# 32-column tiles for layer 0's projections, adapters of experts 0 to 3 in the score banks, and padded FFN weights

## The chip, the cores and the metric

The kernel runs on one core of a Trainium2 chip. The metric is the device time of one execution in microseconds (us), less is better. The time before is the median of three runs; the profile is of one execution.

## The reference

Two post-norm transformer layers on x of 8 batches x 512 tokens x 512 features, all in fp32. Layer 0 has causal attention with 16 heads of 32 and a mixture of 8 experts (top 2 by a router), each with low-rank adapters of rank 16. Layer 1 has an attention with 8 query heads of 64 on 2 key/value heads, and a gated FFN with integer weights, 1408 hidden units.

```python
def _L0_attn_ref(x, WQ_w, WQ_b, WK_w, WK_b, WV_w, WV_b, WO_w, WO_b):
    q = (x @ WQ_w.T + WQ_b).reshape(b, s, NH, HD).transpose(0, 2, 1, 3)    # k and v likewise
    scores = jnp.einsum('bhqd,bhkd->bhqk', q, k) * (1.0 / math.sqrt(HD))
    scores = jnp.where(causal, -jnp.inf, scores)
    out = jnp.einsum('bhqk,bhkd->bhqd', jax.nn.softmax(scores, axis=-1), v)
    return out.transpose(0, 2, 1, 3).reshape(b, s, h) @ WO_w.T + WO_b

def _L0_ffn_ref(x, ...):
    router_logits = xf @ gate_weight.T + xf @ gate_delta.T          # gate_delta = 2 * B @ A
    routing_weights, selected = jax.lax.top_k(softmax(router_logits), 2)    # then normalised to sum 1
    gup = einsum('th,eho->teo', xf, gate_up_proj) + SCALING * einsum('ter,eor->teo', einsum('th,erh->ter', xf, gup_lora_A), gup_lora_B)
    gates, h = jnp.split(gup, 2, axis=-1)
    h = silu(gates) * h
    out = einsum('tei,eih->teh', h, down_proj) + SCALING * (the same with down_lora_A, down_lora_B)
    # the two selected experts' rows of out, weighted and summed

def _L1_ffn_ref(x, wq_gate, s_gate, wq_up, s_up, wq_down, s_down):   # W = (wq - 128) * scale
    return _qlinear(silu(_qlinear(x, wq_gate, s_gate)) * _qlinear(x, wq_up, s_up), wq_down, s_down)

x = layernorm(x + _L0_attn_ref(x, ...))
x = layernorm(x + _L0_ffn_ref(x, ...))
x = layernorm(x + _L1_attn_ref(x, ...))
x = layernorm(x + _L1_ffn_ref(x, ...))
```

## The kernel before

The kernel runs in four stages one after the other: attention of layer 0 (from the start to about 710 us), expert tiles (to about 1200 us), attention of layer 1 (to about 1675 us) and the FFN of layer 1 (to the end). They overlap somewhat at their ends.

**Attention of layer 0** (`attention0`). For each batch b there are four groups g of four heads, and for each group three units u, which take the key tiles {0}, {1, 3} and {2} of 128 keys. We write a unit as (g, u). A unit computes its scores (`scores`, L1386): four matmuls per key tile, one for each head, with 32 rows of weights each, so that each head uses 32 rows of TensorE's array ("32*128" in the profile: rows*columns of the weights). The result `sc` has four PSUM banks, one for each head, and there is one such buffer (`p_sc`, bufs=1). Causality leaves 512 - 128 kt query columns for key tile kt; unit 2 therefore fills 256 of the 512 columns of each bank. ScalarE takes the exponential (L1390), POOL masks the diagonal block (L1395). Then come the unit's other tasks ("thunks", below). Last comes the product with the values of the unit before (`product`, L1410): four matmuls with 32 columns of weights ("128*32"), one for each head, each to its own 32 partitions of `av`. With unit 1 comes `normalise` of the group before: the sums of the exponentials by matmuls with ones (`rs`, L1425, also 128*32), a copy on ScalarE (L1004), reciprocal and product on VectorE (L1428, L1429), a guard's sum on POOL (L1007).

The tasks are set out by `plan(b)`. For a batch in the middle they are values (`value`, L1294) in group 0, query and key (`query` L1301, `key` L1313) of the next group, and the output projection of the batch before (`project`, L1321), each four matmuls that accumulate over 128-row chunks, with 128*128 weights and 512 moving columns. There are also the router's products: `score` (logits, L491), `choose` (L503), `dispatch` (L547, L548) and `enter` (a table of tokens, L588, in bf16). They use two PSUM banks in turn (tag "mm"). For batches 1 to 6 unit (3,2) has, ahead of `score`, one `merge`, and unit (2,2) another.

A `merge` adds the adapters to one 512-column chunk of two experts' weights: two matmuls with 16 rows (`delta`, L781) to two "mm" banks, for each a copy on ScalarE with the factor 2 (`scaled`, L792) and an add on POOL (L794). `scaled` tiles share two buffers with `r_inv` of `normalise`. Of the 24 merges, 12 (experts 0 to 3) lie in batches 1 to 6, and 12 (experts 4 to 7) among the first expert tiles.

The order on TensorE is that of the program only where `in_order` is open: in the first few instructions, and from group 2 of the last batch on. In between, the framework's planner picks for each engine the first instruction of the program that its own estimate of the times calls ready, and a buffer of a tag is chosen when its first writer is planned.

**Attention of layer 1** multiplies in tiles of 64 columns (`Attention1.multiply`, L1600).

**FFN of layer 1** (`IntegerFfn`). For each batch, 11 chunks c of 128 hidden units. Gate and up (`hidden`, L1152) are 16 matmuls with 128*128 weights on two halves of x (a high and a low part in float32r), and down (`out`, L1168) has the hidden halves as weights and the down weights as moving data. The weights, 33 units of 512 columns, lie in two tiles `ffn_w`: the first has 20 units (gate and up of chunks 0 to 9), the second the rest. `IntegerWeights.open` allocates them, the first in the pool `c_weights` on the right side of SBUF, below `x_2` to `x_7`.

In the profile one fp32 matmul of the program is two records; a float32r or bf16 matmul is one.

Of the kernel before, what the change touches and what calls it, by code (L numbers as in the profile page):

```python
# [9 lines left out]
F32 = mybir.dt.float32  # L10
# [8 lines left out]
P = 128  # L19
NB = 8  # L20
# [33 lines left out]
V_BQ, V_BK, V_NS, V_SS, V_SG, V_SU = 0, 4, 8, 12, 16, 16 + NHID  # L54
N_VEC = 16 + 2 * NHID


# [359 lines left out]
class Router:  # L417
# [75 lines left out]

    def choose(self, b, parts, ps):

# [6 lines left out]
        for t in range(NT):  # L502
            nc.tensor.matmul(ps[:, t, :], lhsT=parts[:, ts(t, P)], rhs=self.gather, start=True, stop=True)  # L503
        pr = small.tile([P, NT, E], F32, name="pr")
# [37 lines left out]

    def dispatch(self, b, ps):

        nc, small = self.nc, self.small
        flat = "p t e -> p (t e)"
        nc.tensor.matmul(ps.rearrange(flat), lhsT=self.before, rhs=self.both.rearrange(flat), start=True, stop=False)  # L547
        nc.tensor.matmul(ps.rearrange(flat), lhsT=self.ones, rhs=self.earlier.rearrange(flat), start=False, stop=True)  # L548
        here = slice(NT * b, NT * (b + 1))
        parts = small.tile([P, TOP_K, NT], F32, name="parts")  # L550
        for k in range(TOP_K):
            for of_expert, out in ((ps, self.ranks[:, k, here]), (self.part, parts[:, k, :])):
                mine = small.tile([P, NT, E], F32, name="mine")
                nc.vector.tensor_tensor(mine, of_expert, self.hots[:, k, here, :], ALU.mult)
                nc.vector.tensor_reduce(out, mine, AX.X, ALU.add)
# [26 lines left out]

    def enter(self, ps, low, high, column):

        nc, n = self.nc, TOP_K * NT
        for h, part in enumerate((low, high)):
            for i in range(n):
                nc.tensor.matmul(ps[:, h, :], lhsT=part[:, i, :], rhs=column[:, i, :], start=i == 0, stop=i == n - 1)  # L588
        nc.vector.tensor_tensor(self.table, ps[:, 0, :], self.table, ALU.add)
        nc.vector.scalar_tensor_tensor(self.table, ps[:, 1, :], float(P), self.table, ALU.mult, ALU.add)  # L590
# [160 lines left out]
class Experts:  # L751
# [31 lines left out]
    def chunk(self, e, c, n=1):  # L783
        return self.by_expert[:, e : e + n, 512 * c : 512 * (c + 1)]

    def merge(self, e, c, ps, scaled):
# [436 lines left out]
def attention0(env, guard, keep, routes, experts, dram, p_mm, tiles_ctx):  # L1223
# [8 lines left out]
    with ExitStack() as phase:  # L1232
# [55 lines left out]
        def mm(shape, name):  # L1288
            return p_mm.tile(shape, F32, tag="mm", name=name)

        def value(b, t):
            ps = mm([P, D], "ps_v")
            for c in range(ND):
                nc.tensor.matmul(ps, lhsT=xts[b][:, c, ts(t, P)], rhs=wv[:, c, :], start=c == 0, stop=c == ND - 1)  # L1294
            vs[t] = own.tile([P, D], F32, tag=f"v{t}", name=f"v{t}")
            nc.vector.tensor_tensor(vs[t], ps, row[:, 0, :], ALU.add)

        def query(b, g):
            ps = mm([P, S], "ps_q")
            for c in range(ND):  # L1300
                nc.tensor.matmul(ps, lhsT=wq[:, g, ts(c, P)], rhs=xts[b][:, c, :], start=c == 0, stop=c == ND - 1)  # L1301
            q = own.tile([P, S], F32, tag="q", name="q", bufs=2)
# [7 lines left out]
        def key(b, g):  # L1310
            ps = mm([P, S], "ps_k")
            for c in range(ND):
                nc.tensor.matmul(ps, lhsT=wk[:, g, ts(c, P)], rhs=xts[b][:, c, :], start=c == 0, stop=c == ND - 1)  # L1313
# [4 lines left out]
        def project(b, t):  # L1318
            ps = mm([P, D], "ps_o")
            for c in range(ND):  # L1320
                nc.tensor.matmul(ps, lhsT=aoTs[b][:, c, ts(t, P)], rhs=wo[:, c, :], start=c == 0, stop=c == ND - 1)  # L1321
            nc.vector.tensor_tensor(xs[b][:, t, :], ps, xs[b][:, t, :], ALU.add)
# [38 lines left out]

        def choose(b):
            router.choose(b, logits.pop(b), mm([P, NT, E], "ps_r"))

        def dispatch(b, mm=mm):
            router.dispatch(b, mm([P, NT, E], "ps_rank"))

# [6 lines left out]

        def enter(rows, mm=mm):
            router.enter(mm([P, 2, E * E_TILES], "ps_table"), *rows)

        def scores(b, g, u):
            q, k = heads[b, g]
            sc = p_sc.tile([P, 4, S], F32, tag="sc", name="sc")  # L1380
            width = 0
            for kt in UNITS[u]:
# [6 lines left out]
            p = own.tile([P, 4, width], F32, tag=f"p{u}", name="p", bufs=2 if u == 0 else 1)  # L1389
            nc.scalar.activation(p, sc[:, :, :width], AF.Exp, scale=scale)  # L1390

            at = 0
# [38 lines left out]

        merges = [(e, c) for e in range(0, E, 2) for c in range(UPS)]

# [6 lines left out]
        def plan(b):  # L1440
# [11 lines left out]
            if b:  # L1452
# [10 lines left out]
                if not by_dma:  # L1463
                    todo[2, 2].append(lambda: choose(pb))
                if not last:
                    todo[2, 2 if by_dma else 1].append(merge)
                    todo[3, 2 if by_dma else 1].insert(0, merge)
            if b == 0:
# [75 lines left out]
        one_hot(b - 1, (0, 1))  # L1544
        project(b, 0)
        project(b, 1)
        rows = one_hot(b - 1, (2, 3))
        project(b, 2)
        project(b, 3)
        experts.load(7)  # L1550
        enter(rows)
        for _ in range(2):
# [6 lines left out]
        merge()  # L1559
        choose(b)  # L1560
        tiles.step()
        merge()
        dispatch(b, tiles.aside)
# [4 lines left out]
        enter(rows, tiles.aside)  # L1568
        tiles.of_fixed = router.fixed(routes)
# [7 lines left out]
class Attention1:  # L1577
# [19 lines left out]
    def multiply(self, b, out, lhsT, rhs, c):  # L1597

        for m in (slice(0, self.HD), slice(self.HD, P)) if b else (slice(0, P),):
            self.nc.tensor.matmul(out[m], lhsT=lhsT[:, m], rhs=rhs, start=c == 0, stop=c == ND - 1)  # L1600

# [266 lines left out]
def usual_pass(tc, ins, held_out):  # L1868
    nc = tc.nc
    with ExitStack() as ctx:  # L1870
# [4 lines left out]
        with tc.tile_pool(name="a_mm", bufs=2, space=PSUM) as p_mm, ExitStack() as attn1_ctx:  # L1875
# [339 lines left out]
```

## Time and profile before

| | before |
|---|---|
| median of three runs | 2182.87 us (2181.64 to 2183.12) |
| the profiled execution | 2183.3 us |
| its span | 2181.6 us |
| granted TensorE clock, mean | 0.997 |
| instructions in the span | 25149 |
| busy: TensorE matmul, VectorE, ScalarE, POOL | 2151.6, 1273.8, 627.5, 497.8 us |
| DMA, mean over the span | 89 GB/s |

The span runs from the first to the last instruction of the program; what lies around it belongs to the execution's time. The matmuls of the profile are pipelined: a record lasts longer than it takes to start the next, so records are read by their starts, and the busy time of a group is no price of one. PE is the matmul, PEld its load of weights. A line of the timeline merges neighbours of one kind; its second number is the time from the first one's start to the last one's end. What stands in brackets behind a line is idle time of that engine just before it, and what ended it.

### The profile page before, as it was taken

What the parts mean: (1) busy time and instruction counts of PE and PEld (TensorE: products, weight loads), DVE (VectorE), ACT (ScalarE), POOL (GpSimd) and SP (SyncE); (2) the same over time, 40 slices, a digit from 0 to 9 for tenths busy, and PEclk for the clock granted to TensorE, in tenths of its full rate; (3) what the DMA queues carried; (4) which work ended last, traced back from release to release, by engine and by line L of the source; (5) the groups of instructions that cost most, each with busy time, mean ns of one, the idle gap of its engine ahead of it and who ended that gap; (6) DMA issues with size and microseconds to landing.
All of it is one profiled execution on the core that took longest, in us unless ns stands there. A gap on an engine that the chain in (4) does not pass through costs nothing. (4 is left out here: it accounts for less than half of the span.)

```text
span 2181.6 us, 25149 instructions
## 1 busy us (share of the span) xinstructions
PE 2151.6 (99%) x9694; PEld 1077.7 (49%) x9694; DVE 1273.8 (58%) x2042; ACT 627.5 (29%) x907; POOL 497.8 (23%) x489
## 2 busy tenths in 40 slices
PE   9999999999999999999999999999999999999997
PEld 3334444444444444444443333333334888888876
DVE  3557665675758543324316988889857644555443
ACT  2332323323223231122123333333332232222222
POOL 2332414324233442132015122231211000000000
PEclk9999999999999999999999999999999999999999
DMA  8030302303132328787644121331201311111000
GB/s 304 20 94 4 97 20 78 97 1 97 33 102 78 107 67 232 212 228 207 192 142 157 49 87 58 97 97 39 78 1 44 102 59 58 58 58 58 20 20 21
DMA packets 159971, 194.87 MB, mean 89 GB/s; under 512 B 61011, under 2 KB 101971, under 8 KB 157283
## 3 DMA queue, kind: packets, MB, share of 16 engines
q1 hardware_dynamic: 148560, 157.49, 23.5%
q0 software_dynamic: 10560, 34.61, 5.5%
q8 instruction: 79, 1.29, 0.2%
q10 hardware_dynamic: 722, 1.07, 0.1%
q14 instruction: 50, 0.40, 0.1%
HBM read 123.67 MB, written 69.47 MB: 89 GB/s over the span
## 5 line engine op out<-in xcount | busy, mean ns | idle before, releaser
L903 PE MATMUL ps_gu<-experts,xrT 128*128 128x512 f32 (+1 forms) x520 | 247.2, 598 | 0.0
L1390 ACT ACTIVATE p<-sc 128x2048 f32<-128x2048 f32 (+1 forms) x96 | 152.9, 1592 | 162.2 <-PE sc L1386 135.8
L1157 DVE SCALAR_TENSOR_TENSOR hT<-ps_u,vec,sg 128x512 f32<-128x512 f32 x88 | 65.6, 745 | 194.6 <-PE ps_u L1152 194.6
L1395 POOL TENSOR_SCALAR_AFFINE_SELECT p<-p 128x512 f32<-128x512 f32 x128 | 92.4, 734 | 360.3 <-ACT p L1390 316.8
L1168 PE MATMUL ps_f<-ffn_w,h_half 128*128 128x512 f32 x672 | 170.3, 393 | 0.6 <-issue 0.4
L1007 POOL TENSOR_TENSOR g_total<-g_total,r_inv 128x512 f32<-128x512 f32 x64 | 89.6, 1400 | 343.7 <-DVE r_inv L1778 272.2
L1418 DVE TENSOR_TENSOR p<-p 128x1536 f32<-128x1536 f32 (+2 forms) x96 | 131.1, 1365 | 46.0 <-POOL p L1395 41.0
L1748 ACT ACTIVATE p<-sc 128x1024 f32<-128x1024 f32 x128 | 124.0, 1021 | 100.4 <-PE sc L1745 95.9
L905 DVE TENSOR_TENSOR h<-ps_gu,h 128x256 f32<-128x256 f32 x67 | 28.4, 424 | 208.8 <-ACT h L904 208.8
L1778 DVE RECIPROCAL r_inv<-r_inv 128x512 f32<-128x512 f32 x32 | 107.1, 3346 | 69.3 <-ACT r_inv L1004 69.3
L1168 PEld LDWEIGHTS ps_f<-ffn_w,h_half 128*128 128x128 f32 x672 | 124.3, 188 | 33.1 <-DVE h_half L1163 5.6
L903 PEld LDWEIGHTS ps_gu<-experts,xrT 128*128 128x128 f32 x520 | 95.8, 196 | 89.3 <-issue 89.0
L1152 PE MATMUL ps_g<-x_high,ffn_w 128*128 128x512 f32 x352 | 138.8, 394 | 0.9 <-DVE x L1719 0.9
L1152 PE MATMUL ps_g<-x_low,ffn_w 128*128 128x512 f32 x352 | 139.0, 395 | 0.0
L1152 PE MATMUL ps_u<-x_low,ffn_w 128*128 128x512 f32 x352 | 138.7, 394 | 0.0
L1152 PE MATMUL ps_u<-x_high,ffn_w 128*128 128x512 f32 x352 | 138.6, 394 | 0.0
L919 PE MATMUL ps_y<-experts,hT 128*128 128x512 f32 (+1 forms) x272 | 128.0, 593 | 0.5 <-ACT hT L913 0.5
L1745 PE MATMUL sc<-qT,kT 64*128 64x512 f32 x512 | 127.2, 615 | 1.0 <-ACT qT L1653 0.7
L1301 PE MATMUL ps_q<-experts 128*128 128x512 f32 x256 | 120.7, 613 | 4.8 <-DMA experts<-in_xT 4.5
L1767 PE MATMUL av<-p,v 128*64 128x512 f32 x512 | 120.9, 593 | 0.0
L1313 PE MATMUL ps_k<-experts 128*128 128x512 f32 x256 | 117.5, 602 | 0.0
L1600 PE MATMUL ps_o<-attn_out,aoT 128*64 128x512 f32 x512 | 116.4, 598 | 0.8 <-ACT r_inv L1004 0.8
(267 smaller groups left out, 3359.6 us busy)
## 6 DMA issues: line engine op xcount, KB each, us to landing
results<-y SPq DMA_DIRECT2D x68, 256.0 KB, 2.2
turned<-turned SPq DMA_DIRECT2D x56, 256.0 KB, 4.1
pair<-xrT SPq DMA_DIRECT2D x25, 512.0 KB, 2.9
xrT<-pair SPq DMA_DIRECT2D x100, 128.0 KB, 4.3
x<-in_x SPq DMA_DIRECT2D x8, 1024.0 KB, 8.5
experts<-in_gate_up SPq DMA_DIRECT2D x8, 1024.0 KB, 11.0
rows<-x SPq DMA_DIRECT2D x32, 256.0 KB, 2.3
x<-rows SPq DMA_DIRECT2D x8, 1024.0 KB, 16.2
```

The costliest lines, as they stand in the source:

```text
L903: nc.tensor.matmul(ps, lhsT=xT[:, c, :], rhs=self.weights(i, c), start=c == 0, stop=c == ND - 1)
L919: self.nc.tensor.matmul(ps, lhsT=hT[:, c, :], rhs=self.weights(i, ND + c), start=c == 0, stop=c == self.NI - 1)
L1152: nc.tensor.matmul(ps, lhsT=w[:, ts(dc, P)], rhs=x[:, dc, :], start=(dc, i) == (0, 0), stop=(dc, i) == (ND - 1, 1))
L1168: self.nc.tensor.matmul(os[t], lhsT=h[:, ts(t, P)], rhs=self.weights(2 * NHID + c), start=(c, i) == (0, 0), stop=(c, i) == (NHID - 1, 1))
L1301: nc.tensor.matmul(ps, lhsT=wq[:, g, ts(c, P)], rhs=xts[b][:, c, :], start=c == 0, stop=c == ND - 1)
L1313: nc.tensor.matmul(ps, lhsT=wk[:, g, ts(c, P)], rhs=xts[b][:, c, :], start=c == 0, stop=c == ND - 1)
L1390: nc.scalar.activation(p, sc[:, :, :width], AF.Exp, scale=scale)
L1418: nc.vector.tensor_tensor(total[:, :, P * kt :], total[:, :, P * kt :], p[:, :, at : at + w], ALU.add)
L1600: self.nc.tensor.matmul(out[m], lhsT=lhsT[:, m], rhs=rhs, start=c == 0, stop=c == ND - 1)
L1745: nc.tensor.matmul(sc[:, j, :], lhsT=st["kT"][hs, ts(kt, P)], rhs=st["qT"][g][hs, :], start=True, stop=True)
L1748: nc.scalar.activation(p, sc, AF.Exp, scale=scale)
L1767: nc.tensor.matmul(st["av"][HD * j : HD * (j + 1), :], lhsT=st["v"][:, kt, HD * j : HD * (j + 1)], rhs=p[:, j, :], start=kt == 0, stop=kt ...
```

## The change

1. A helper splits a matmul into products of `columns` columns of the weights, each to its own partitions of the result. `value`, `query`, `key` and `project` use it with 32 columns, except for `project` of the last batch's own rows, which comes after the heads. So do `choose`, `dispatch` and `enter`, except for their last calls (`enter` for the last two batches, `choose` and `dispatch` for the last).
2. The adapters of experts 0 to 3 are no longer merged by `merge`. In batches 1 to 6, units (2,2) and (3,2) multiply half a chunk (256 columns) for all four experts into the free columns 256 to 511 of the score banks, ahead of their scores. After the exponential two copies on ScalarE, of two experts each, and two adds on POOL follow. Units (2,2) and (3,2) lose their `merge`.
3. The pool of the first FFN weight tile gets a second tile of 224 bytes per partition, which nothing uses.

```diff
+def matmul_by_columns(nc, out, lhsT, rhs, start=True, stop=True, columns=32):
+    for at in range(0, P, columns):
+        m = slice(at, at + columns)
+        nc.tensor.matmul(out[m], lhsT=lhsT[:, m], rhs=rhs, start=start, stop=stop)

     def choose(self, b, parts, ps, columns):
...
         for t in range(NT):
-            nc.tensor.matmul(ps[:, t, :], lhsT=parts[:, ts(t, P)], rhs=self.gather, start=True, stop=True)
+            matmul_by_columns(nc, ps[:, t, :], parts[:, ts(t, P)], self.gather, columns=columns)

     def dispatch(self, b, ps, columns):
...
-        nc.tensor.matmul(ps.rearrange(flat), lhsT=self.before, rhs=self.both.rearrange(flat), start=True, stop=False)
-        nc.tensor.matmul(ps.rearrange(flat), lhsT=self.ones, rhs=self.earlier.rearrange(flat), start=False, stop=True)
+        matmul_by_columns(nc, out, self.before, self.both.rearrange(flat), stop=False, columns=columns)
+        matmul_by_columns(nc, out, self.ones, self.earlier.rearrange(flat), start=False, columns=columns)

     def enter(self, ps, low, high, column, columns):
...
-                nc.tensor.matmul(ps[:, h, :], lhsT=part[:, i, :], rhs=column[:, i, :], start=i == 0, stop=i == n - 1)
+                matmul_by_columns(nc, ps[:, h, :], part[:, i, :], column[:, i, :], i == 0, i == n - 1, columns)

+    def delta_halves(self, ps, c, half):
+        for e in range(4):
+            a, bt = lora_factors(self.lora[32 * e : 32 * e + R, :], c)
+            self.nc.tensor.matmul(ps[:, e, :], lhsT=a, rhs=bt[:, 256 * half : 256 * (half + 1)], start=True, stop=True)
+
+    def merge_halves(self, ps, c, half, scaled):
+        for e, two in zip((0, 2), scaled):
+            two = two.rearrange("p (e f) -> p e f", e=2)
+            self.nc.scalar.mul(two, ps[:, e : e + 2, :], LORA_SCALE)
+            w = self.chunk(e, c, 2)[:, :, 256 * half : 256 * (half + 1)]
+            self.nc.gpsimd.tensor_tensor(w, w, two, ALU.add)

+        def multiply(out, lhsT, rhs, c):
+            matmul_by_columns(nc, out, lhsT, rhs, start=c == 0, stop=c == ND - 1)
...
             for c in range(ND):
-                nc.tensor.matmul(ps, lhsT=wq[:, g, ts(c, P)], rhs=xts[b][:, c, :], start=c == 0, stop=c == ND - 1)
+                multiply(ps, wq[:, g, ts(c, P)], xts[b][:, c, :], c)
...
+        def project(b, t, out_of_heads=False):
...
+                (wide if out_of_heads else multiply)(ps, aoTs[b][:, c, ts(t, P)], wo[:, c, :], c)

         def scores(b, g, u):
...
+            beside = halves.pop(0) if u == 2 and g >= 2 and 0 < b < NB - 1 else None
+            if beside:
+                experts.delta_halves(sc[:, :, S - 256 :], *beside)
...
             nc.scalar.activation(p, sc[:, :, :width], AF.Exp, scale=scale)
+            if beside:
+                scaled = [work.tile([P, 512], F32, tag="r_inv", name="scaled", bufs=2) for _ in range(2)]
+                experts.merge_halves(sc[:, :, S - 256 :], *beside, scaled)

-        merges = [(e, c) for e in range(0, E, 2) for c in range(UPS)]
+        halves = [(c, half) for c in range(UPS) for half in range(2)]
+        merges = [(e, c) for e in range(4, E, 2) for c in range(UPS)]
...
-                if not last:
-                    todo[2, 2 if by_dma else 1].append(merge)
-                    todo[3, 2 if by_dma else 1].insert(0, merge)
...
-        enter(rows)
+        enter(rows, columns=P)
...
-            weights.open(ctx.enter_context(tc.tile_pool(name="c_weights", bufs=1, side="right")), weights.FIRST)
+            pool = ctx.enter_context(tc.tile_pool(name="c_weights", bufs=1, side="right"))
+            weights.open(pool, weights.FIRST)
+            pool.tile([P, 56], F32, name="c_aligned")
```

More of the change, by code (lines that the diff above doesn't have):

```diff
@@ L492, in logits, with choose @@
                                   start=True, stop=True)
-    def choose(self, b, parts, ps):
+    def choose(self, b, parts, ps, columns):
         nc, small = self.nc, self.small
@@ L541, in choose, with dispatch @@
         nc.vector.tensor_tensor(self.carry, self.earlier[:, NT - 1, :], self.both[:, NT - 1, :], ALU.add)
-    def dispatch(self, b, ps):
+    def dispatch(self, b, ps, columns):
         nc, small = self.nc, self.small
         flat = "p t e -> p (t e)"
-        nc.tensor.matmul(ps.rearrange(flat), lhsT=self.before, rhs=self.both.rearrange(flat), start=True, stop=False)
-        nc.tensor.matmul(ps.rearrange(flat), lhsT=self.ones, rhs=self.earlier.rearrange(flat), start=False, stop=True)
+        out = ps.rearrange(flat)
+        matmul_by_columns(nc, out, self.before, self.both.rearrange(flat), stop=False, columns=columns)
+        matmul_by_columns(nc, out, self.ones, self.earlier.rearrange(flat), start=False, columns=columns)
         here = slice(NT * b, NT * (b + 1))
@@ L581, in one_hot, with enter @@
         return low, high, column
-    def enter(self, ps, low, high, column):
+    def enter(self, ps, low, high, column, columns):
         nc, n = self.nc, TOP_K * NT
@@ L1293, in value @@
             for c in range(ND):
-                nc.tensor.matmul(ps, lhsT=xts[b][:, c, ts(t, P)], rhs=wv[:, c, :], start=c == 0, stop=c == ND - 1)
+                multiply(ps, xts[b][:, c, ts(t, P)], wv[:, c, :], c)
             vs[t] = own.tile([P, D], F32, tag=f"v{t}", name=f"v{t}")
@@ L1312, in key @@
             for c in range(ND):
-                nc.tensor.matmul(ps, lhsT=wk[:, g, ts(c, P)], rhs=xts[b][:, c, :], start=c == 0, stop=c == ND - 1)
+                multiply(ps, wk[:, g, ts(c, P)], xts[b][:, c, :], c)
             k = own.tile([P, S], F32, tag="k", name="k", bufs=2)
@@ L1316, in key, with wide @@
             heads[b, g].append(k)
-        def project(b, t):
+        def wide(out, lhsT, rhs, c):
+            nc.tensor.matmul(out, lhsT=lhsT, rhs=rhs, start=c == 0, stop=c == ND - 1)
+        def project(b, t, out_of_heads=False):
             ps = mm([P, D], "ps_o")
             for c in range(ND):
-                nc.tensor.matmul(ps, lhsT=aoTs[b][:, c, ts(t, P)], rhs=wo[:, c, :], start=c == 0, stop=c == ND - 1)
+                (wide if out_of_heads else multiply)(ps, aoTs[b][:, c, ts(t, P)], wo[:, c, :], c)
             nc.vector.tensor_tensor(xs[b][:, t, :], ps, xs[b][:, t, :], ALU.add)
@@ L1360, in score, with choose, dispatch @@
                 nc.scalar.copy(logits[b], ps)
[L1362 to L1366, printed above, removed]
+        def choose(b, columns=HD):
+            router.choose(b, logits.pop(b), mm([P, NT, E], "ps_r"), columns)
+        def dispatch(b, mm=mm, columns=HD):
+            router.dispatch(b, mm([P, NT, E], "ps_rank"), columns)
         rooms = {}
@@ L1373, in one_hot, with enter @@
             return router.one_hot(b, rooms[b], places)
-        def enter(rows, mm=mm):
-            router.enter(mm([P, 2, E * E_TILES], "ps_table"), *rows)
+        def enter(rows, mm=mm, columns=HD):
+            router.enter(mm([P, 2, E * E_TILES], "ps_table"), *rows, columns)
         def scores(b, g, u):
@@ L1544, in attention0 @@
         one_hot(b - 1, (0, 1))
-        project(b, 0)
-        project(b, 1)
+        project(b, 0, True)
+        project(b, 1, True)
         rows = one_hot(b - 1, (2, 3))
-        project(b, 2)
-        project(b, 3)
+        project(b, 2, True)
+        project(b, 3, True)
         experts.load(7)
-        enter(rows)
+        enter(rows, columns=P)
         for _ in range(2):
@@ L1559, in attention0 @@
         merge()
-        choose(b)
+        choose(b, P)
         tiles.step()
         merge()
-        dispatch(b, tiles.aside)
+        dispatch(b, tiles.aside, P)
         for places in ((0, 1), (2, 3)):
@@ L1567, in attention0 @@
             merge()
-        enter(rows, tiles.aside)
+        enter(rows, tiles.aside, P)
         tiles.of_fixed = router.fixed(routes)
@@ L1597, in multiply @@
     def multiply(self, b, out, lhsT, rhs, c):
-        for m in (slice(0, self.HD), slice(self.HD, P)) if b else (slice(0, P),):
-            self.nc.tensor.matmul(out[m], lhsT=lhsT[:, m], rhs=rhs, start=c == 0, stop=c == ND - 1)
+        matmul_by_columns(self.nc, out, lhsT, rhs, c == 0, c == ND - 1, self.HD if b else P)
     def prepare(self, b):
```

## The prediction

> **What bounds the kernel now.** I read the page's table of engines and its 40 slices first, then the order of TensorE's matmuls around one unit of layer 0, then the same in layer 1 and in the FFN, and last ScalarE and POOL around a merge.
>
> ```profile
> PE 2151.6 (99%) x9694; PEld 1077.7 (49%) x9694; DVE 1273.8 (58%) x2042; ACT 627.5 (29%) x907; POOL 497.8 (23%) x489
> ...
> PE   9999999999999999999999999999999999999997
> ```
>
> TensorE is busy in every slice and no other engine passes 58%: time taken out of TensorE's own stream is gained, up to the point where another engine makes it wait. Busy time doesn't say whether TensorE runs well, so I read the starts. The timeline of PE for units (2,1) to (3,0) of one batch (start us, us, line, tile, rows*columns of weights, xcount):
>
> ```profile
> 322.98 1.07 PE L1410 MATMUL av<-p,v 128*32 128x512 f32 x8
> 323.86 1.04 PE L1425 MATMUL rs<-p,ones 128*32 128x512 f32 x8
> 324.83 0.71 PE L1386 MATMUL sc<-q,k 32*128 32x256 f32 x8
> 325.48 3.70 PE L1313 MATMUL ps_k<-experts 128*128 128x512 f32 x8
> 329.11 1.97 PE L781 MATMUL ps_lora<-lora 16*128 16x512 f32 x4
> 331.00 1.07 PE L1410 MATMUL av<-p,v 128*32 128x384 f32 x16
> 332.01 1.14 PE L1386 MATMUL sc<-q,k 32*128 32x512 f32 x8
> 333.08 3.70 PE L1301 MATMUL ps_q<-experts 128*128 128x512 f32 x8
> 336.71 0.64 PE L1410 MATMUL av<-p,v 128*32 128x256 f32 x8
> ```
>
> One fp32 matmul is two records. In the run 128*128 records start 0.429 us apart (ps_k: 8 x 0.429 = 3.43), and a round of four 32-column records, one for each quarter of the array, starts 0.429 after the last (av, 2 rounds: 0.88): **the four overlap wholly**, for the same product. But ps_k takes 3.63, av to rs 0.88, rs to sc 0.97 for 0.86 of rounds. The excess sits where the shape of the tile changes. Split up by its starts: 0.11 on each change between 32*128 and another shape (0.095 from 128*128 to 128*32 and from 32*128 to 128*32), and behind it, on the second load of weights, 0.104 for 128*128, 0.107 for 32*128 and only 0.024 for 128*32.
>
> Layer 1 already multiplies in 64-column tiles, with one moving operand for both:
>
> ```profile
> 1240.99 3.65 PE L1600 MATMUL ps_k<-hT,attn_qkv 128*64 128x512 f32 x16
> 1244.48 1.89 PE L1767 MATMUL av<-p,v 128*64 128x512 f32 x8
> ...
> 1249.07 3.71 PE L1600 MATMUL ps_v<-attn_qkv,hT 128*64 128x128 f32 x64
> 1252.61 0.60 PE L1600 MATMUL ps_q<-hT,attn_qkv 128*64 128x512 f32 x2
> ```
>
> 16 records take 3.49, that is 8 rounds of 0.429 and 0.05 for the entry, and av follows with no change. ps_v passes 64 matmuls and 64 loads in 3.54: 28 ns an instruction can be issued over a long stretch.
>
> In the FFN, chunk 9 and chunk 10 of a batch, first records and what follows:
>
> ```profile
> 1726.47 0.39 PE L1152 MATMUL ps_g<-x_high,ffn_w 128*128 128x512 f32 x1
> ...
> 1730.20 1.98 PE L1168 MATMUL ps_f<-ffn_w,h_half 128*128 128x512 f32 x8
> 1732.01 0.39 PE L1152 MATMUL ps_g<-x_high,ffn_w 128*128 128x512 f32 x1
> ...
> 1735.64 2.46 PE L1168 MATMUL ps_f<-ffn_w,h_half 128*128 128x512 f32 x10
> ```
>
> 16 records in 3.73 (233 ns each) against 3.63 (227 ns), and so in the seven batches that run chunk 10 in one piece. Chunks 0 to 9 read gate and up weights from the first weight tile, chunk 10 from the second. By the program's allocation the first begins at byte 138720 of a partition, 224 over a multiple of 256, the second at 92416, a multiple of 256.
>
> **What the Trainium skill says.** "TensorEngine Tiling (Array Packing)", Tiling Modes: a change of tiling mode drains TensorE. The trace agrees, at about 0.1 us a change. "TensorE: Matmul & The Clock Gate", Part 3: column tiles run at the same time, starting some 4 ns apart; the trace shows 7 ns, and full overlap. The first page, Performance Considerations, warns that a matmul with few moving columns has a fixed cost[...]: no 32-column product of 8 columns is in this trace. "PSUM — Partial Sum Buffer", on bank collisions: a bank's quadrant that one engine reads can't be written by another. So scores can't go into a bank whose other half ScalarE still reads; no run here shows a collision, only waits. No page I found prices the 224 bytes.
>
> **The change part by part**, against the profiled execution, 2183.3 us (span 2181.6 and 1.7 around it); the median of the runs is 0.4 lower.
>
> (a) Projections, 128*128 to 128*32. The rounds stay at 0.429. A run between sc and av costs now 0.110 + 0.104 on entry and 0.095 + 0.024 on leaving, 0.333; then 0.094 + 0.024 on entry and nothing towards av, 0.118. Saved: 0.215 a run. Batches 1 to 6 have 11 such runs (one in each of 12 units but the last): 2.37 x 6 = 14.2. Batch 0 has about 12, some split, 2.5; batch 7 keeps 128*128 transposes among them, about 1.0. Sum **-17.7**. All of it is on TensorE.
>
> (b) Merges of experts 0 to 3 leave units (2,2) and (3,2). The first costs 331.00 - 329.11 = 1.90; the second, next to sc, 4 x 0.429 = 1.72: 6 x 3.62 = 21.7. In their place 8 records of 256 columns, four row tiles at once as in sc (2 x 0.213 = 0.43), same shape as the scores behind them, so no change of shape: 12 x 0.43 = 5.2. **-16.5**. ScalarE's two copies and POOL's two adds per merge stay in number, only earlier. No DMA moves; SP's queue is untouched.
>
> (c) Small products. Now, without the change of shape: choose 0.77 (8 records), dispatch 0.34 (4), enter 1.72 (16 of bf16). After, 32, 16 and 64 matmuls with as many loads. At 13.6 ns an instruction (av of 128 columns passes 16 instructions in 0.217) 0.87, 0.44 and 1.74; at ps_v's 28 ns, 1.8, 0.9 and 3.6. Below nothing too: loads of 32 columns last 0.11 against 0.19, so choose could halve. Over 7, 7 and 6 batches: -3.5 to +22. I take **+3**, near the burst[...].
>
> (d) The score bank is held longer. The ACT timeline of a unit (3,2), and after it POOL's:
>
> ```profile
> 344.62 1.02 ACT L1390 ACTIVATE p<-sc 128x1024 f32<-128x1024 f32 x1
> 345.54 0.59 ACT L792 ACTIVATE scaled<-ps_lora 128x512 f32<-128x512 f32 x1
> 348.82 0.60 ACT L792 ACTIVATE scaled<-ps_lora 128x512 f32<-128x512 f32 x1 [2.69 <-POOL experts L794]
> ```
>
> ```profile
> 347.51 1.27 POOL L794 TENSOR_TENSOR experts<-experts,scaled 128x512 f32<-128x512 f32 x1
> ```
>
> The second copy waited for POOL, as `scaled` shares two buffers with r_inv and one is r_inv's. Today that holds a projection bank; afterwards the score bank, of which there is one. After (3,2) TensorE has only logits (0.98 with the entry) and av (0.85) before the next scores, due at 346.7 on this clock. The copies: scores end at 345.0, exp (1.02) 346.0, first copy 346.6, POOL's add (1.27, behind the mask of 0.63 to 1.83) 348.1 to 348.8, second copy 348.7 to 349.4: a wait of 2.1 to 2.8. At (2,2) key lies between (3.43), and the wait is 0.45: counted from the sc at 324.83, the scores are due at 330.3, the second copy ends at 330.0, k's bias (0.69) stands behind it in ScalarE's queue, and the scores wait for k. Uncovered: 6 x 2.4 + 6 x 0.45, about 17, at most 20. But PE's order in batches 1 to 6 is the planner's: in batch 0 it put half of a ps_q (4 records at 43.10) ahead of scores whose bank was busy. Here the values of the next batch could go ahead, 6.9 us in the same shape. Half covered: **+8.5** (0 to 20). POOL's mask may wait behind an add, 1.3 to 1.9; its product comes behind 3.4 us of query or 6.9 of values, and that hides it.
>
> (e) Padding. Pools on that side grow downwards (x_2 begins at 179680, where the weights end), so 224 bytes move the first tile to 138496, a multiple of 256: 10 chunks x 16 x 8 = 1280 records at 6.5 ns less, **-8.3**. Nothing else in the stage ends later than TensorE (its share there is 100%). Bounds: 0, if the address isn't the cause, to -8.5.
>
> Instruction fetch grows with some 3,600 matmul records and their loads; its queues now have 0.2% and 0.1%, hidden.
>
> Sum: -17.7 - 16.5 + 3 + 8.5 - 8.3 = -31.0: 2152.3 for a profiled execution, **2152** for the median.
>
> **Rivals.** *All covered*: (d) is 0 and (c) 1.4: 2142. For it: batch 0's order. *Nothing covered*: the planner thinks the bank free too early, (d) 17 to 20 and (c) 5: 2163 to 2166. For it: POOL's adds last 1.27 to 2.26 by what DVE does beside them, which a plan may not know. *The pad does nothing*: 233 ns has another cause, 2160. Against it: down products, all from the second tile, also show 226. *Slower*: **rounds of four cost more than 0.429** in the projections, as a common moving operand or 8 instructions a round hold up issue. There are 992 rounds (256 each for q, k, v, 224 for o); from 31 ns a round the gain is gone, from 36 it is slower by 0.2%. Were loads as dear as the 62 ns that the clock-gate page (Part 1) gives for a firmware-decoded matmul, a round would last 8 x 62 = 496: an estimate of +66, 2218. Against it: 28 ns an instruction in ps_v, and pairs with a common operand in ps_k.
>
> **How the numbers follow.** Half covered 0.55, all covered 0.20, nothing covered 0.14, pad inert 0.06, slower 0.05. 0.2% of 2183 is 4.4 us, about what a measurement can tell from no change. The range, 2139 to 2167, takes the first four; beyond it are dear small products together with no cover, and the slower case. Faster 0.93, same 0.03, slower 0.04.
>
> **What would show it.** TensorE's records near 13,260 (9694 + 2976 + 540 + 48). ps_q, ps_k, ps_v, ps_o as 128*32 with 8 rounds in 3.43 to 3.55 and av right behind; no L781 between batches 1 and 6; sc with 256 columns 0.43 longer at (2,2) and (3,2); waits of PE's sc for the copies between 0 and 2.8; all FFN records 227 apart. Rounds over 0.44, choose over 1.8, or an FFN still at 233 would prove me wrong.

## The result, and the profile after

The changed kernel is slower: 2206.46 us (median of five runs, 2206.18 to 2210.64) against 2182.47, a ratio of 1.0113 with a 95% interval of 1.0098 to 1.0128. The forecast was 2152. The profiled execution took 2206.46, its span is 2204.7, and the mean granted TensorE clock fell from 0.997 to 0.989. Lines move with the diff; those used below are the helper for 32 columns L62, scores L1417, exponential L1421, mask L1429, av L1444, p add L1452, rs L1459, reciprocal L1462, aoT L1463, the guard's sum of inverses L1029, half deltas L798, their copies L804 and adds L806, k's bias L1340, FFN gate and up L1174, down L1190.

The page's table of engines and the first row of its slices, after:

```profile
PE 2130.9 (97%) x13258; PEld 1018.3 (46%) x13258; DVE 1283.6 (58%) x2042; ACT 628.3 (28%) x907; POOL 487.6 (22%) x489
...
PE   9999898999989999999999999999999999999997
```

TensorE has 13,258 records, as forecast, and 20.7 us less busy time, yet the span grew by 23.1. In the slices the nines have holes, all in the first third, in layer 0. The timeline of PE for units (2,1) to (3,0) of batch 3, the ones shown for before:

```profile
332.03 1.04 PE L1444 MATMUL av<-p,v 128*32 128x512 f32 x8
332.89 1.04 PE L1459 MATMUL rs<-p,ones 128*32 128x512 f32 x8
333.86 0.71 PE L798 MATMUL sc<-lora 16*128 16x256 f32 x8
334.39 0.61 PE L1417 MATMUL sc<-q,k 32*128 32x256 f32 x8
334.94 3.64 PE L62 MATMUL ps_k<-experts 128*32 128x512 f32 x32
338.39 1.05 PE L1444 MATMUL av<-p,v 128*32 128x384 f32 x16
343.67 2.09 PE L1417 MATMUL sc<-q,k 32*128 32x512 f32 x8 [4.23 <-ACT k L1340]
345.69 4.13 PE L62 MATMUL ps_q<-experts 128*32 128x512 f32 x32
349.65 0.60 PE L1444 MATMUL av<-p,v 128*32 128x256 f32 x8
```

The TensorE part of the forecast is there. ps_k's 8 rounds take 3.45 from start to start (334.94 to 338.39, before 3.63), av follows without a change of shape, delta and scores take 1.08 together, and the merge of 1.90 is gone. Then two things that were not forecast in this size: **a wait of 4.23 us** in front of the next scores, and behind it scores that last 2.02 from start to start (343.67 to 345.69) where before they lasted 1.07, and a ps_q of 3.96 (345.69 to 349.65) where other runs of this shape take 3.46. The table of PE's waits (total, times, longest), after:

```profile
PE sc L1417 <- ACT k L1340: 26.2, 7, 4.3
PE sc L1417 <- ACT scaled L804: 17.2, 6, 2.9
```

Each of batches 1 to 6 has both: 4.2 behind (2,2) and 2.9 behind (3,2), by the gaps between records 6 x 7.1 = 42.7 us in all. Who is late is read from three timelines of the same stretch, ScalarE's, POOL's and VectorE's:

```profile
335.07 1.02 ACT L1421 ACTIVATE p<-sc 128x1024 f32<-128x1024 f32 x1 [0.39 <-PE sc L1417]
335.99 0.59 ACT L804 ACTIVATE scaled<-sc 128x512 f32<-128x512 f32 x1
342.44 0.60 ACT L804 ACTIVATE scaled<-sc 128x512 f32<-128x512 f32 x1 [5.85 <-POOL g_total L1029]
342.94 0.68 ACT L1340 ACTIVATE k<-ps_k,vec 128x512 f32<-128x512 f32 x1
```

```profile
340.83 1.58 POOL L1029 TENSOR_TENSOR g_total<-g_total,r_inv 128x512 f32<-128x512 f32 x1 [8.58 <-DVE r_inv L1462]
342.37 0.63 POOL L1429 TENSOR_SCALAR_AFFINE_SELECT p<-p 128x512 f32<-128x512 f32 x1
342.97 3.48 POOL L806 TENSOR_TENSOR experts<-experts,scaled 128x512 f32<-128x512 f32 x2
```

```profile
335.77 1.71 DVE L1452 TENSOR_TENSOR p<-p 128x1536 f32<-128x1536 f32 x1
337.41 3.34 DVE L1462 RECIPROCAL r_inv<-r_inv 128x512 f32<-128x512 f32 x1
```

The first copy runs as soon as the exponential is through. The second waits 5.85 us, k's bias stands behind it in ScalarE's queue, and the scores wait for k. POOL's sum, which releases the copy, waits in its turn for a reciprocal of 3.34 us.

The stretch behind the wait, as windows with the granted clock (the third number from the end; ahead of it the busy time and count of each engine, behind it DMA):

```profile
338.40:343.30 4.90, 1.04 (x20) 0.39 (x12) 3.76 (x4) 0.86 (x2) 2.47 (x3) 1.00 0.93 196
343.30:346.70 3.40, 3.03 (x16) 0.87 (x20) 2.01 (x1) 1.19 (x2) 3.14 (x2) 0.50 1.03 308
346.70:360.00 13.30, 13.30 (x146) 4.66 (x138) 4.85 (x3) 6.25 (x8) 6.38 (x4) 1.00 0.39 150
```

For 3.4 us after the wait the clock is at 0.50; we call this a stretch at half clock. There are ten of them between 90 and 660 us, 37.5 us together, and none in the kernel before.

### The profile page after: what moved, and what is told of

Read it like the earlier page. It is cut to its first block, busy times and chain, and to the rows that moved or that the text cites. A ratio compares the mean times of both kernels' runs of the same rounds, so it can differ in the third digit from the quotient of the medians.

```text
span 2204.7 us, 32282 instructions
## 1 busy us (share of the span) xinstructions
PE 2130.9 (97%) x13258; PEld 1018.3 (46%) x13258; DVE 1283.6 (58%) x2042; ACT 628.3 (28%) x907; POOL 487.6 (22%) x489
## 3 DMA queue, kind: packets, MB, share of 16 engines
q8 instruction: 107, 1.75, 0.3%
q10 hardware_dynamic: 722, 1.07, 0.1%
## 5 line engine op out<-in xcount | busy, mean ns | idle before, releaser
L1421 ACT ACTIVATE p<-sc 128x2048 f32<-128x2048 f32 (+1 forms) x96 | 152.9, 1593 | 182.9 <-PE sc L1417 159.2
L1029 POOL TENSOR_TENSOR g_total<-g_total,r_inv 128x512 f32<-128x512 f32 x64 | 90.2, 1409 | 406.5 <-DVE r_inv L1808 271.9
L1190 PE MATMUL ps_f<-ffn_w,h_half 128*128 128x512 f32 x672 | 169.7, 393 | 2.7 <-DVE h_half L1185 2.0
L1452 DVE TENSOR_TENSOR p<-p 128x1536 f32<-128x1536 f32 (+2 forms) x96 | 141.4, 1473 | 48.6 <-PE av L1444 34.5
L1429 POOL TENSOR_SCALAR_AFFINE_SELECT p<-p 128x512 f32<-128x512 f32 x128 | 82.4, 655 | 349.6 <-ACT p L1421 291.1
L1417 PE MATMUL sc<-q,k 32*128 32x512 f32 (+3 forms) x1024 | 98.6, 477 | 45.9 <-ACT k L1340 26.2
L1190 PEld LDWEIGHTS ps_f<-ffn_w,h_half 128*128 128x128 f32 x672 | 124.4, 188 | 34.8 <-DVE h_half L1185 7.7
L1174 PE MATMUL ps_g<-x_high,ffn_w 128*128 128x512 f32 x352 | 137.2, 390 | 0.9 <-DVE x L1749 0.9
L1174 PE MATMUL ps_g<-x_low,ffn_w 128*128 128x512 f32 x352 | 137.0, 389 | 0.0
L1174 PE MATMUL ps_u<-x_high,ffn_w 128*128 128x512 f32 x352 | 136.9, 389 | 0.0
L1174 PE MATMUL ps_u<-x_low,ffn_w 128*128 128x512 f32 x352 | 136.9, 389 | 0.0
L925 PEld LDWEIGHTS ps_gu<-experts,xrT 128*128 128x128 f32 x520 | 95.2, 195 | 88.9 <-issue 88.7
L62 PE MATMUL ps_q<-experts 128*32 128x512 f32 x1024 | 128.9, 635 | 5.0 <-DMA experts<-in_xT 4.7
L62 PE MATMUL ps_v<-experts 128*32 128x512 f32 x1024 | 127.1, 621 | 0.0
```

Source lines behind the costliest of these rows:

```text
L62: nc.tensor.matmul(out[m], lhsT=lhsT[:, m], rhs=rhs, start=start, stop=stop)
L925: nc.tensor.matmul(ps, lhsT=xT[:, c, :], rhs=self.weights(i, c), start=c == 0, stop=c == ND - 1)
L1174: nc.tensor.matmul(ps, lhsT=w[:, ts(dc, P)], rhs=x[:, dc, :], start=(dc, i) == (0, 0), stop=(dc, i) == (ND - 1, 1))
L1190: self.nc.tensor.matmul(os[t], lhsT=h[:, ts(t, P)], rhs=self.weights(2 * NHID + c), start=(c, i) == (0, 0), stop=(c, i) == (NHID - 1, 1))
L1417: nc.tensor.matmul(sc[:, j, width : width + w], lhsT=k[hs, ts(kt, P)], rhs=q[hs, P * kt :], start=True, stop=True)
L1452: nc.vector.tensor_tensor(total[:, :, P * kt :], total[:, :, P * kt :], p[:, :, at : at + w], ALU.add)
```

## The experiments

Two measures are given for each: the whole time, with its ratio to runs of the kernel before and the 95% interval, and the sum of batches 1 to 6, from the first scores of batch 1 to those of batch 7 in the trace (before 533.5 us, after 566.1).

**1. Merges as before.** Only the adapter part is undone.

```diff
-            beside = halves.pop(0) if u == 2 and g >= 2 and 0 < b < NB - 1 else None
+            beside = None
...
-        merges = [(e, c) for e in range(4, E, 2) for c in range(UPS)]
+        merges = [(e, c) for e in range(0, E, 2) for c in range(UPS)]
...
+                if not last:
+                    todo[2, 2 if by_dma else 1].append(merge)
+                    todo[3, 2 if by_dma else 1].insert(0, merge)
```

> The changed kernel with the adapters of experts 0 to 3 merged as before (whole chunks to projection banks, units (2,2) and (3,2)); 32-column products and padding stay. Theory (the score bank is held by the second copy, which waits for POOL): no wait of scores over 0.5 us, no half-clock window between 80 and 640 us, mean clock 0.996, about 2166 us (2162 to 2171). Rival (the 32-column products themselves cost time or draw the clock down): clock 0.990 or less, 2195 us or more.

Measured: 2162.57, ratio 0.9908 (0.9892 to 0.9925); batches 1 to 6 520.8; no half-clock stretch between 90 and 660 us. The expectation held: 32 columns and padding gain 20 us, the adapters, as the changed kernel has them, cost 44.

**2. The adapters alone.** The kernel before with the adapter part, every product at 128 columns, no padding.

```diff
-            matmul_by_columns(nc, out, lhsT, rhs, start=c == 0, stop=c == ND - 1)
+            matmul_by_columns(nc, out, lhsT, rhs, start=c == 0, stop=c == ND - 1, columns=P)
```

(and columns=P for choose, dispatch and enter, and no tile `c_aligned`).

> The kernel before with the adapter part alone: products for the score banks' free halves, but all projections and router products 128 columns wide, no padding. Theory: scores wait some 3.9 us after (2,2) and 2.7 after (3,2) in each of six batches, each wait is followed by a half-clock window, about 2220 us (2212 to 2228). Rival (32-column products are to blame): the adapter part gains its 16 us, 2165 to 2172.

Measured: 2228.59, ratio 1.0211 (1.0194 to 1.0228), just over the expected span; waits of 3.69 and 2.65, batches 1 to 6 578.4. The loss does not need the 32-column products.

**3. The half merges in groups 0 and 1.**

```diff
-            beside = halves.pop(0) if u == 2 and g >= 2 and 0 < b < NB - 1 else None
+            beside = halves.pop(0) if u == 2 and g < 2 and 0 < b < NB - 1 else None
```

> The changed kernel with the half merges in units (0,2) and (1,2), where 7.8 and 9.5 us of other TensorE work lie between these scores and the next. Theory: the second copy ends some 8.1 us after the scores as before, so (1,2) has no wait and (0,2) one of about 0.9 us (the key's bias stands behind the copy on ScalarE); no half-clock windows; about 2153 us (2146 to 2160). Rival (sharing the score bank costs wherever it is put): 2200 us or more.

Measured: 2168.35, ratio 0.9939 (0.9923 to 0.9956), batches 1 to 6 527.1: faster than the changed kernel by 38, but 15 short of the expectation. The waits moved to other tiles:

```profile
PE ps_table L62 <- ACT k L1340: 10.9, 5, 2.2
...
PE av L1444 <- POOL p L1429: 4.4, 4, 1.6
```

k's bias, again behind the second copy, here holds a projection bank that enter's `ps_table` needs. The copy had waited 6.39 us, this time by the trace for POOL's add; in group 0, where the copy waits 3.3 us for g_total, other work covers it. Three of these waits are followed by a stretch at half clock.

**4. Without the guard's sum.** Theory at this point: POOL's adds are late because POOL, in its planned order, has to wait for the reciprocal in g_total first. The kernel leaves layer 0's inverses out of the guard's total.

```diff
             nc.vector.tensor_tensor(aoTs[b][:, g, :], av, r_inv, ALU.mult)
-            guard.watch_inverses(r_inv)
```

> The changed kernel without the guard's sum of inverses on POOL in layer 0 (left out: that sum alone, which only decides on a fallback). Theory (the first add stands behind that sum in POOL's queue, and so behind VectorE's reciprocal): the wait after (2,2) falls from 4.2 to about 0.4 us, after (3,2) it stays at 1.5 to 2.5 us; about 2174 us (2166 to 2182). Rival (the second copy waits for VectorE or for the r_inv buffer itself): within 3 us of the changed kernel, 2203 to 2209.

Measured: 2196.69, ratio 1.0065 (1.0048 to 1.0082), batches 1 to 6 556.5, waits of 3.7 and 2.35; the time lies between the two expectations. This theory fell. POOL's first add now ran early, at once after the mask, and the copy waited all the same (ScalarE's timeline, then POOL's):

```profile
333.43 0.60 ACT L804 ACTIVATE scaled<-sc 128x512 f32<-128x512 f32 x1
339.35 0.60 ACT L804 ACTIVATE scaled<-sc 128x512 f32<-128x512 f32 x1 [5.33 <-DVE aoT L1463]
```

```profile
335.38 1.28 POOL L806 TENSOR_TENSOR experts<-experts,scaled 128x512 f32<-128x512 f32 x1
```

If the copy needed the buffer of the first copy, it could have gone at 336.7, when the add had read it. It went after aoT, the last reader of r_inv that is left. So it waits for **r_inv's own buffer**. The timelines of the changed kernel, above, already spoke against this theory: there the second copy starts at 342.44, ahead of POOL's first add, at 342.97, so it can't have waited for that add.

**5. Another buffer for the second copy at (2,2).**

```diff
-                scaled = [work.tile([P, 512], F32, tag="r_inv", name="scaled", bufs=2) for _ in range(2)]
+                scaled = [work.tile([P, 512], F32, tag="r_inv", name="scaled", bufs=2)]
+                if g == 2:
+                    scaled.append(work.tile([P, 512], F32, tag="logits", name="scaled_l"))
+                else:
+                    scaled.append(work.tile([P, 512], F32, tag="r_inv", name="scaled", bufs=2))
```

> The changed kernel with one edit: at (2,2) the second of the two scaled copies goes to the buffer of the logits, free at that point, instead of the two buffers that r_inv rotates through; at (3,2) everything stays. Theory (the second copy waits for r_inv's own buffer, held until reciprocal, aoT product and the guard's sum are through): the 4.2 us wait of the scores after (2,2) goes in each of batches 1 to 6 and with it the stretch at half clock behind it, 6 x (4.2 + 1.4) = 34 us: 2172 (2168 to 2178), and the 2.9 us wait after (3,2) stays. Rival (ACT's copies are late whatever the buffer, because the adds on POOL or the k bias stand behind something else): the wait stays at 3 us or more, 2195 to 2206.

Measured: 2199.87, ratio 1.0084 (1.0068 to 1.0099), batches 1 to 6 553.6. On the cause the theory held: no wait is left behind (2,2). On the time it missed, for the wait behind (3,2) doubled, and brought a stretch at half clock of 6.83 us in each batch. PE's waits, and POOL's timeline ahead of (3,2):

```profile
PE sc L1417 <- ACT scaled L804: 35.1, 6, 5.8
```

```profile
342.90 4.56 POOL L1548 TENSOR_TENSOR x<-x,row 128x2048 f32<-128x2048 f32 x1 [0.57 <-DMA x<-in_x]
347.40 1.24 POOL L1433 TENSOR_SCALAR_AFFINE_SELECT p<-p 128x512 f32<-128x512 f32 x2
353.66 1.51 POOL L1029 TENSOR_TENSOR g_total<-g_total,r_inv 128x512 f32<-128x512 f32 x1 [5.02 <-DVE r_inv L1466]
```

With TensorE no longer held up, the add of the bias row to x, 4.56 us long and started by a load, lies ahead of two masks. VectorE's p add, which waits for them, starts at 348.08; its reciprocal behind that starts at 350.17, 2.0 after the first copy at 348.20 (in the changed kernel 1.1 ahead of it: 357.58 and 358.69). r_inv's buffer comes free 3 us later, and the copy, which still needs it at (3,2), waits 5.84 instead of 2.87. This too says what the copy waits for.

**6. Another buffer at both places.** The second copy at (3,2) goes to the buffer of x1T, which the logits have just read, and the copies stand behind the logits in the program.

```diff
+                def copies(sc=sc, beside=beside):
+                    scaled = [work.tile([P, 512], F32, tag="r_inv", name="scaled", bufs=2)]
+                    if g == 2:
+                        scaled.append(work.tile([P, 512], F32, tag="logits", name="scaled_l"))
+                    else:
+                        scaled.append(work.tile([P, ND, S], F32, tag="x1T", name="scaled_x")[:, 0, :])
+                    experts.merge_halves(sc[:, :, S - 256 :], *beside, scaled)
...
                 todo[(3, 2) if by_dma else (2, 1)].append(lambda: score(pb))
+                if by_dma:
+                    todo[3, 2].append(lambda: held.pop()())
```

> The changed kernel with the second copy at (2,2) in the logits' buffer and the one at (3,2) in the buffer of x1T, free once the logits' products have read it (so that copy is issued behind the logits). No copy then waits for a buffer of r_inv. Theory (the whole loss is that wait, twice in each batch, and the stretch at half clock behind it): the batch falls from 95.2 to 95.2 - 7.1 - 2.9 = 85.2 us, six times, so 2206.5 - 60 = 2147; with a microsecond for what else may be late, 2149 (2145 to 2156), no PE wait over 1 us and no half-clock stretch in batches 1 to 6, and under the 2162.6 of the same kernel with the merges as before. Rival (POOL's four adds and two sums for each batch, in one planned order with the masks and the add of the output's row, become the next limit, as they did when only the first wait was taken away): a wait of 2 to 5 us for POOL's masks or for the av bank, 2165 to 2185.

Measured: **2155.39**, ratio 0.9879 (0.9862 to 0.9895), batches 1 to 6 511.5. The theory held: ScalarE's timeline at (2,2) has the copies back to back, k's bias waits for nothing but its own product, and the next scores on PE start with no wait:

```profile
317.73 0.59 ACT L804 ACTIVATE scaled<-sc 128x512 f32<-128x512 f32 x1
318.20 0.60 ACT L804 ACTIVATE scaled_l<-sc 128x512 f32<-128x512 f32 x1
320.38 0.69 ACT L1340 ACTIVATE k<-ps_k,vec 128x512 f32<-128x512 f32 x1 [1.57 <-PE ps_k L62]
```

```profile
320.12 1.05 PE L1454 MATMUL av<-p,v 128*32 128x384 f32 x16
321.12 1.14 PE L1417 MATMUL sc<-q,k 32*128 32x512 f32 x8
```

There is no half-clock stretch between 90 and 660 us. ScalarE's order at (3,2) is the same in both traces (first copy, copy of the logits, second copy), so what differs there is the buffer and not the place in the program. Other buffers for the second copies, at two places of a batch, are worth 51.1 us (2206.46 - 2155.39), and this version is faster than both kernels.

**7. Half merges at (2,2) only,** the second copy in the logits' buffer, the other half of the chunks merged as before at (3,2).

```diff
+            beside = halves.pop(0) if u == 2 and g == 2 and 0 < b < NB - 1 else None
...
+        halves = [(c, half) for c in range(UPS // 2) for half in range(2)]
+        merges = [(e, c) for e in range(0, E, 2) for c in range(UPS) if e > 2 or c >= UPS // 2]
...
+                if not last:
+                    todo[3, 2 if by_dma else 1].insert(0, merge)
```

> The changed kernel with half merges in the score banks at (2,2) only, the second copy in the logits' buffer, and the other half of the chunks of experts 0 to 3 merged as before at (3,2). Theory: without a buffer to wait for, six half merges cost 6 x 0.43 us and take away half of the merges' 21.7: 2162.6 - 10.9 + 2.6 = 2154 (2150 to 2159), no wait over 1 us after (2,2) and no stretch at half clock. Rival (the longer hold of the bank costs more than the merge even without the buffer, through k's bias behind two copies): 2163 to 2175.

Measured: 2164.34, ratio 0.9924 (0.9909 to 0.9939), batches 1 to 6 519.0: nothing gained on experiment 1, and the theory missed by 10 us. The time is the rival's, the reason is not: there is no wait behind (2,2), but at (3,2) the merge's second copy waits 3.5 to 4.4 us for POOL's add, and holds a projection bank that the next values need, for 1.1 to 2.0 us in each of six batches. One of these waits (1.97) has a stretch at half clock behind it.

```profile
PE ps_v L62 <- ACT scaled L814: 9.6, 6, 2.0
```

**8. The padding alone.**

```diff
+            pool.tile([P, 56], F32, name="c_aligned")
```

> The kernel before with the padding of the FFN weights alone (56 columns ahead of the ring's end, as in the changed kernel). Theory: the padding is worth what the FFN stage was seen to shrink by in the changed kernel's trace, 492.6 to 486.4 us, so 6.2 us off the 2182.5 of before: 2176.3 (2175 to 2178). The forecast's own step said 8.3: 2174.2. Rival (the stage shrank for another reason, such as another order of its loads): within 1 us of before.

Measured: 2177.09, ratio 0.9975 (0.9966 to 0.9983), so 5.6 us; batches 1 to 6 533.5, as before. The theory held. Where the other 2 us of the forecast's 8.3 went is below.

**9. Small products at 128 columns,** on experiment 1.

```diff
-        def choose(b, columns=HD):
+        def choose(b, columns=P):
...
-        def dispatch(b, mm=mm, columns=HD):
+        def dispatch(b, mm=mm, columns=P):
...
-        def enter(rows, mm=mm, columns=HD):
+        def enter(rows, mm=mm, columns=P):
```

> The changed kernel with the merges as before and with choose, dispatch and enter at 128 columns: only projections and padding are left of the change, beside 2162.6 for the same with the small products at 32 columns. The forecast put +3 us on the small products: 2159.6. Rival (the 32-column small products spare changes of the array's shape and pay for themselves, as enter's 64 records in 1.75 us suggest): 2162.5 to 2168.

Measured: 2167.85, ratio 0.9934 (0.992 to 0.9947), batches 1 to 6 526.8 against 520.8. The rival held: 32 columns save 5 to 6 us here. PE's timeline at choose, first at 128 columns, then at 32 (experiment 1):

```profile
264.34 1.06 PE L62 MATMUL ps_r<-r_gather,logits 128*128 128x8 f32 x8
265.32 0.64 PE L1444 MATMUL av<-p,v 128*32 128x256 f32 x8
```

```profile
262.60 0.44 PE L62 MATMUL ps_r<-r_gather,logits 128*32 128x8 f32 x31
262.88 0.40 PE L1444 MATMUL av<-p,v 128*32 128x256 f32 x1
```

8 records take 0.98 with the change of shape behind them; 32 records take 0.28.

**10. Batch 0's cut queries at 128 columns,** on experiment 6.

```diff
-                multiply(ps, wq[:, g, ts(c, P)], xts[b][:, c, :], c)
+                (wide if (0, 1) < (b, g) < (1, 1) else multiply)(ps, wq[:, g, ts(c, P)], xts[b][:, c, :], c)
```

> The kernel of e10 (both second copies in other buffers) with three queries, (0,2), (0,3) and (1,0), at 128 columns again: the ones that the planned order cuts into 10, 19 and 3 records in the middle of rounds of four. Theory (batch 0 gained nothing because a cut round costs whole rounds): the stretch from such a query to the scores after rs was 7.311 us against 6.761 before, so batch 0 (first scores to first scores) falls from 68.11 by 3 x 0.55 to 66.5, less some 0.1 each at av; the whole 2155.4 - 1.5 = 2153.9. Rival (something else fills batch 0, such as the loads): 68.1 and 2155.4.

Measured: 2154.12, ratio 0.9867 (0.985 to 0.9883), 1.3 below experiment 6, which is within the spread of the runs. In the trace batch 0 fell from 68.11 to 66.80, that is by 3 x 0.55 less the 3 x 0.11 for av, as the theory has it. Batches 1 to 6 were 1.4 longer (512.9), for which I have no reason. Batch 0's query in the changed kernel, PE's timeline:

```profile
56.37 1.88 PE L62 MATMUL ps_q<-experts 128*32 128x512 f32 x10
58.18 1.15 PE L1417 MATMUL sc<-q,k 32*128 32x384 f32 x16
59.25 2.35 PE L62 MATMUL ps_q<-experts 128*32 128x512 f32 x19
61.02 0.59 PE L1444 MATMUL av<-p,v 128*32 128x512 f32 x1
61.42 0.61 PE L62 MATMUL ps_q<-experts 128*32 128x512 f32 x3
```

The plan cuts it after 5 of 16 matmuls, one round of four and one quarter: 10 records, then 22. The first piece takes 1.81 where 2.5 rounds are 1.07. The second is out of step with the columns: single records of av and rs start among its last ones and among one another, until the scores.

## Why the prediction was wrong

| step | forecast | measured | from |
|---|---|---|---|
| (a) + (c) projections, small products | -14.7 | -14.5 | experiment 1 against 8 |
| (b) merges to half merges | -16.5 | -7.2 | 6 against 1 |
| (d) score bank held longer | +8.5 | +51.1 | after against 6 |
| (e) padding | -8.3 | -5.4 | 8 against before (2182.47) |
| sum | -31.0 | +24.0 | |

**(d) is the step that failed**, and it fails in one sentence: "POOL's add (1.27, behind the mask of 0.63 to 1.83) 348.1 to 348.8, second copy 348.7 to 349.4". It let the second copy take over the first copy's buffer, as the trace of before had it at (3,2) ("[2.69 <-POOL experts L794]"), and carried that over to (2,2). The same paragraph names the other buffer, "one is r_inv's", and doesn't ask when that one is released: not before reciprocal (3.34), aoT (0.68) and the sum on POOL (1.58). In the changed kernel the copy gets it at both places. So 0.45 at (2,2) became 4.2, and 2.1 to 2.8 at (3,2) became 2.87. Experiments 4, 5 and 6 settle the buffer: with POOL's add early the wait stays; with another buffer it goes, at one place and then at both.

The trace of before had this wait at (2,2), in all six batches. ScalarE's timeline, before:

```profile
333.08 0.60 ACT L792 ACTIVATE scaled<-ps_lora 128x512 f32<-128x512 f32 x1 [2.17 <-POOL g_total L1007]
```

This second copy starts 8.25 after the scores at 324.83; in the changed kernel it is 8.05 (334.39 to 342.44). An estimate from this line: k's bias, 0.5 behind the copy and 0.69 long, ends at 334.3, where the scores were due at 330.3. That is a wait of 4.0 in place of 0.45.

That the size at (3,2) came near is luck, for there too g_total released the copy, not the add. ScalarE's timeline, after:

```profile
362.62 0.60 ACT L804 ACTIVATE scaled<-sc 128x512 f32<-128x512 f32 x1 [2.87 <-POOL g_total L1029]
```

The forecast's sum is also short at its upper end: an exponential until 346.0, a mask of 1.83 and an add of 1.27 give 349.1 and not 348.8, so a wait of up to 3.1.

Two terms were missing beside it. Of the cover, "half covered", nothing was seen: at (3,2) the plan put one 32-column matmul of the next values ahead of the scores, not 6.9 us of them. And no step priced what a wait does to the clock. After minus experiment 6 is 54.6 us over batches 1 to 6. TensorE's idle time, by the gaps between its records, is 42.7 us in the one and 4.3 in the other, so 38.3 of it; some 16 are left for the ten stretches at half clock, a little under half of their 37.5. A batch with both waits and one stretch of 3.41 took 93.37, where the four batches with two such stretches took 95.1 to 95.2. The rival *nothing covered* had the place and the sign of this, with 17 to 20 where 51 was true.

**(a) and (c)** came out right as a sum by luck, and wrong as parts. The rounds of four stay at 0.429, so the rival that they cost more fell. (c) was +3 and is a saving, of 5.3 by experiment 9: in experiment 1 choose takes 0.28 for the forecast 0.87, dispatch 0.12 for 0.44. The four column tiles of a product overlap here too, and no change of shape is left. Enter, at 1.75, was right. That leaves 9.2 for (a), where 17.7 stood (experiment 9 against 8). It gained nothing in batch 0 (68.20 before, 68.11 after) where 2.5 stood: "some split" was named and not priced. In experiment 9 the merges and the wide small products keep changes of shape beside the projections; how much of the rest that explains stays open.

**(b)** has its prices right: delta takes 0.54 where the forecast had 0.43, and the merges' 22 us went (by starts 6 x 3.74 in experiment 1). But in experiment 6, too, the plan puts one matmul of the next values ahead of the scores at (3,2). By starts the values of a batch come to 8.70 (0.95 and 7.74, a wait of 0.68 for a bank that choose needs in it) against 6.89 in experiment 1: 1.8 a batch, 10.8 in all. A matmul moved ahead as cover cuts a round of four, as in batch 0.

**(e)** was right in its cause. Chunk 9 and what follows, PE's timeline after:

```profile
1755.07 0.39 PE L1174 MATMUL ps_g<-x_high,ffn_w 128*128 128x512 f32 x1
...
1758.69 1.98 PE L1190 MATMUL ps_f<-ffn_w,h_half 128*128 128x512 f32 x8
```

16 records in 3.62, as in every chunk. But "nothing else in the stage ends later than TensorE" no longer held: the hidden halves come late at seven places, where before it was 0.2 at one. PE's waits, after:

```profile
PE ps_f L1190 <- DVE h_half L1185: 2.0, 7, 0.5
```

So the stage shrank by 6.2 (492.6 to 486.4) instead of 8.3. Experiment 8, with the padding alone, has the same seven waits of 2.0 together.

## What to carry to other kernels

When work moves to another point of a loop, ask of every buffer that it writes who holds it at the new point and until when, for each copy of a rotating buffer by itself, and read the releaser at every place of the loop: here it was the add at one and g_total at the other. A wait that looks like a queue (g_total on POOL) and one for a buffer show the same releaser. See whether the waiting instruction starts ahead of the one that it is said to need, or take the suspected instruction out and see whether the wait stays. Splitting a product into column tiles paid here where the plan kept the rounds whole; batch 0, where it cut them, gained nothing.

## What the runs showed of the hardware that was not expected

**A wait on TensorE costs twice.** The Trainium skill ("TensorE: Matmul & The Clock Gate", Part 1, What's actually happening) says that a free-running window of some 3.4 us decides on the clock, and that after an idle one it runs at half. The traces agree: every stretch lasts 3.41 or 6.83 us, and those of a run start whole multiples of 3.41 apart. The page's limit is one idle window; here shorter gaps are enough. Gaps in TensorE's records between 90 and 660 us, in the traces of before, after and the ten experiments:

| gap, us | gaps | followed by half clock |
|---|---|---|
| 3.7 to 5.9 | 24 | 24 |
| 2.6 to 2.9 | 11 | 9 |
| 1.9 to 2.4 | 13 | 5 |
| 0.8 to 1.7 | 14 | 0 |

No stretch at half clock lies there without such a gap before it. Gaps of one length go both ways because it matters how they fall on the windows. The starts of the stretches mark a grid of 3.41 us in each trace; counted on it, the idle time within one window, by the records, sorts the windows at full clock almost without an overlap:

| idle in a window, us | windows | followed by half clock |
|---|---|---|
| under 1.8 | 1903 | 0 |
| 1.8 to 2.0 | 8 | 6 |
| over 2.0 | 32 | 32 |

At half clock, the 38 windows with up to 0.34 us idle were the last of their stretch, and the 11 with 0.74 or more were followed by another. So in these traces about 1.9 us of idle time in one window, and not a whole one, brought the clock down. No run moved the gaps and nothing else: this is a count over twelve traces, not an experiment of its own.

**Small column tiles are cheap when they come in fours.** The 32 records of choose in experiment 1 start within 0.28 us, 9 ns apart. The clock-gate page of the Trainium skill, "Wait — 56ns, not 53.3ns?" in Part 1, gives some 25 ns as the least distance of two matmuls; for neighbours in different columns the trace shows a third of it. From one round of four to the next it is 28 to 33 ns, so no quarter of the array starts more often than the page has it. Enter's 64 records, of 256 bf16 columns, take 1.75, 27 ns each.
